# A two-layer transformer with cross-attention and a mixture of experts on one core: the plan of the side work rearranged

## The chip, the core and the metric

The kernel runs on one core of a Trainium2 chip. Such a core has five engines, each with a queue of its own that is worked off in order: TensorE (PE in the profile, its weight loads PEld), VectorE (DVE), ScalarE (ACT), GpSimd (POOL) and SyncE (SP), whose queue here issues DMAs. The metric is the device time of one execution in microseconds, the median of several runs; lower is better.

## The reference

64 sequences of 32 rows with 256 features (2048 rows in all), and a context of 257 rows for each sequence. Six steps, each added to `x` after a layer norm, cut to what matters:

```python
x = x + xattn0(norm(x), ctx)   # 16 heads of 16, rotary, window: first 32 context rows, causal
x = x + attn0(norm(x))         # 16 heads of 16, rotary, causal over the 32 rows
x = x + ffn0(norm(x))          # 256 -> 256, input rounded to fp8 with one scale a row
x = x + xattn1(norm(x), ctx)   # 16 heads, all 257 context rows, masked
x = x + attn1(norm(x))         # "mixer", below
x = x + moe(norm(x))           # 1 shared and 8 routed experts, 256 -> 512 -> 256, top 2

def mixer(x):
    gate = sigmoid(relu(x @ gate_w1 + b1) @ gate_w2 + b2)          # 64, then 32 features
    glob = gate * (x @ U_w) * cumsum(x @ V_w, axis=1)
    return conv3(x) + glob @ out_w + out_b

def moe(h):
    probs = softmax(h @ router_w + router_b)                       # 8 logits a row
    w = top-2 probs of a row, others 0
    return shared(h) + sum_e w[e] * expert_e(h)
```

## The kernel before

**Tiles.** The rows lie in SBUF as four groups `xs[g]` of four tiles of 128 rows (`NG = NT = 4`); a tile is four sequences. There are three stages: the two small attentions of layer 0 (to about 197 us), the big cross-attention of layer 1 (to about 688 us), and `mixture`, the experts with their routing.

**How order is made.** Inside the cross-attention and around it the engines' queues follow the order in which the Python code issues instructions, so the plan written out in the code is the plan that runs. The steps of side work (`linear`, `norm_steps`, `mixer`, `normed`) are generators: each `yield` ends a piece, and somebody calls `next` on them between the pieces of the main work. Work that is put off a little further goes to a list, `pending`, which `catch_up()` empties.

**The cross-attention's loop** (`cross_attention`, L1400 to L1459) runs over tiles `i` = 0 to 17 and pieces `b` = 0 to 3; the text calls one piece a tick, k = 4i + b. Three tiles are in flight: the keys of tile i+1, the scores of tile i, and values and context of tile i−1. A tick issues, in this order: four transposes `ps_t` and their copy `eT`; the weights' products put off from the tick before (POOL), `own_heads` and, at b = 1, `project` (`ps_p`); `catch_up()`; `run(k − 0.5)`; eight matmuls of values `ps_v`; four more `ps_t`; one piece of `side`; `run(k)`; `head_blocks` (`qb`, POOL) for a later tile and the keys `ps_k`; the scores `ps_s` in two halves, followed by four minima on the DVE (`e<-ps_s,mask`) and four exponentials on ACT; at b = 1 `last_keys` (`ps_le`, then `lv`); the context `ps_o`. A tick without side work lasts 5.67 us on PE.

**The side work of the loop** is `side_work(g + 1)`, begun at t = 0 of each group: the nine pieces of `linear` (norm, row maxima, scaling by the reciprocal, rounding to fp8 in two pairs with a helper tile `big`, sums `y`, `q`, transposes `ps_qT` in `by_feature`, matmuls `ps_ff` in `outputs`), the norm of the cross-attention, its transposes `psT`, and two matmuls of queries `ps_q`. `linear` of group 0 and the norm behind it are run by `first_sides()` between the last groups of layer 0 (L1481).

**The planned work.** `planned()` (L1032) puts the pieces of the mixers of finished groups and of the norms before the experts (`normed`: norm, store of `y` for the gathers, transposes `psT`, router matmuls `ps_r` of 8 columns, `lg`) at ticks. A mixer's pieces: statistics, two halves of the norm with `y` by ACT, transposes `psT`, the product `ps_huv` with the scan and product that make `hub` on the DVE, the gate `ps_g`, two `ps_d` with their convolution taps (`conv`), and two pairs of rows transposed back, `ps_x`, and added to `x`. A rank-one part of each norm, the reciprocal root, is a chain of twelve short instructions on POOL; the last ones use `eng = vector`, the DVE.

**PSUM.** All side tiles of the cross-attention (`ps_k`, `ps_v`, `ps_le`, `ps_p`, `psT`, `ps_qT`, `ps_ff`, `ps_q`, `ps_huv`, `ps_g`, `ps_d`, `ps_x`, `ps_r`) take turns in two banks through `shared_bank`: each waits for the reader of the tile before the last.

**The mixture** (L1526) issues the last mixer half (`mixer(3, range(2, 4), vector, False)`), the norms of group 3, the routing (`choose`) of the first 12 tiles and of the last 4, matmuls of the shared expert between them (`ps_sh`, `ps_so`), and then the 20 expert tiles. `last_pieces` holds what the plan leaves over: before, one norm, that of the first half of group 3.

Of the kernel before, what the change touches and what calls it, by code (L numbers as in the profile page):

```python
# [20 lines left out]
NG, NT = 4, 4  # L21
# [44 lines left out]
def perceiver_kernel(ctx: ExitStack, tc: tile.TileContext, a: dict, out: bass.AP):  # L66
# [619 lines left out]
    def catch_up():  # L686
        while pending:
            pending.pop(0)()

    def linear(g, by_act=False):  # L690

        x = xs[g]
        y = yield from norm_steps(g)

        for t in range(NT // 2):
            gpsimd.tensor_tensor(x[:, t], x[:, t], row(R_FF), ALU.add)
        yield
        am = small.tile([P, NT], F32, tag="am", name="am")
        vector.tensor_reduce(am, y, AX.X, ALU.max, apply_absolute_value=True)
        xsc = small.tile([P, NT], F32, tag="xsc", name="xsc")  # L700
        rsc = small.tile([P, NT], F32, tag="rsc", name="rsc")
        osc = small.tile([P, NT], F32, tag="osc", name="osc")

        def scales():
            vector.tensor_scalar(xsc, am, 1e-12, 1.0 / 448.0, ALU.max, ALU.mult)
            vector.reciprocal(rsc, xsc)
            vector.tensor_scalar(osc, xsc, vec[:, V_WS : V_WS + 1], None, ALU.mult)

        pending.append(scales)
        for t in range(NT // 2, NT):  # L710
            gpsimd.tensor_tensor(x[:, t], x[:, t], row(R_FF), ALU.add)
        yield

        def scaled(ts):
            for t in ts:
                if by_act:
                    scalar.activation(y[:, t], y[:, t], AF.Copy, scale=rsc[:, t : t + 1])
                else:
                    gpsimd.tensor_scalar(
                        y[:, t], y[:, t], rsc[:, t : t + 1], 1.0, ALU.mult, ALU.mult  # L720
                    )

        scaled(range(2 if by_act else NT))
        yield
        qs, qTs = [], []

        def rounded(pair):


            v = y[:, 2 * pair : 2 * pair + 2, :]  # L730
            big = sb.tile([P, 2, D], F32, tag="big", name="big")
            vector.tensor_scalar(
                big.bitcast(I32), v.bitcast(I32), 0x7F800000, None, ALU.bitwise_and
            )
            vector.tensor_scalar(big, big, 2.0**-6, 1.5 * 2.0**20, ALU.max, ALU.mult)
            q = sb.tile([P, 2, D], BF16, tag=f"fq{pair}", name="q")
            qs.append(q)

            def sums():
                vector.tensor_tensor(v, v, big, ALU.add)  # L740
                vector.tensor_tensor(q, v, big, ALU.subtract)

            pending.append(sums)

        def by_feature(pair):
            ps = shared_bank[0]([P, 2, 2 * P], "ps_qT", BF16)
            for c in range(2):
                for i in range(2):
                    turn(ps[:, c, i * P : (i + 1) * P], qs[pair][:, i, c * P : (c + 1) * P], ident_bf)
            qT = sb.tile([P, 2, 2 * P], BF16, tag=f"fqT{pair}", name="qT8")  # L750
            scalar.copy(qT, ps)
            qTs.append(qT)

        def outputs(pair):
            ps = shared_bank[0]([P, 2, D], "ps_ff")
            for i in range(2):
                proj(
                    ps[:, i, :],
                    lambda k: qTs[pair][:, k, i * P : (i + 1) * P],
                    lambda k: w8[:, k, :],  # L760
                )
            for i in range(2):
                t = 2 * pair + i
                x = xs[g][:, t, :]
                vector.scalar_tensor_tensor(
                    x, ps[:, i, :], osc[:, t : t + 1], x, ALU.mult, ALU.add
                )

        rounded(0)
        if by_act:  # L770
            scaled(range(2, NT))
        yield
        rounded(1)
        yield
        by_feature(0)
        yield
        by_feature(1)
        outputs(0)
        yield
        outputs(1)  # L780

# [11 lines left out]
    def mixer(g, ts, eng=None, by_act=True, early=False):  # L793
# [4 lines left out]
        steps = norm_steps(g, eng, True, ts, by_act, lent[:, 1] if early else None)  # L798
# [66 lines left out]
        for pair in range(n // 2):  # L865
            ps = shared_bank[0]([P, 2, D], "ps_x")
            for i in range(2):
                at = slice((2 * pair + i) * P, (2 * pair + i + 1) * P)
                for c in range(2):
                    turn(ps[:, i, c * P : (c + 1) * P], conv[c][:, at], ident)  # L870
            mine = x[:, t0 + 2 * pair : t0 + 2 * pair + 2, :]
            vector.tensor_tensor(mine, ps, mine, ALU.add)


    nt_all = NG * NT
# [145 lines left out]
    def fill_hidden(n):  # L1021

        for _ in range(n):
            shared_hidden(*next(hidden_units))
# [7 lines left out]
    def planned():  # L1032
        def at(piece, *turns):
            for k in turns:
                plan.setdefault(k, []).append(lambda: next(piece, None))

        plan[5] = [
            lambda: vector.tensor_scalar(
                half_b[64:96], vec[64:96, V_GB2 : V_GB2 + 1], 0.5, None, ALU.mult
            )  # L1040
        ]
        for g in range(2):
            k = 16 * g
            at(
                mixer(g, range(NT), early=True),
                *range(k + 24, k + 31), k + 33, k + 34, k + 36,
            )
        at(mixer(2, range(NT)), 53, 54, 55, 55, 56, 57, 58, 59, 60, 61)
        at(normed(0, range(NT)), 48, 51, 52, 54, 57, 58)
        at(normed(1, range(NT)), 56, 58, 59, 60, 62, 63)  # L1050
        at(mixer(3, range(2)), 60.5, 61, 62, 63, 64, 65, 66, 67)
        plan.setdefault(66, []).append(lambda: fill_hidden(1))
        at(normed(2, range(NT)), 62, 63, 64, 65, 66, 67)
        plan[65].append(lambda: fill_hidden(1))
        plan[66].append(lambda: fill_hidden(2))
        last_pieces.append(normed(3, range(2)))

    def run(k):
# [3 lines left out]
    last_pieces = []  # L1062


    def cross_attention(loaded):
# [28 lines left out]
        def key_tile(i):  # L1094
# [4 lines left out]

        own4 = fold[:, None, :].to_broadcast([P, 8, S])  # L1100
        of4 = sb.tile([P, 4, DH], F32, tag="of4", name="of4")
        vector.tensor_copy(
            of4, cst[:, C_B4 : C_B4 + 4][:, :, None].to_broadcast([P, 4, DH])
        )

# [3 lines left out]
        def last_rows(i, dst):  # L1109
            ps = pkv([P, 2, NB], "ps_l")  # L1110
            for c in range(2):
                proj(
                    ps[:, c, :],
                    lambda k: w[:, i, k, c * P : (c + 1) * P],
                    lambda k: lasts[:, k, :],
                )
            if i == 1:
                bias = vec[:, V_X1K : V_X1K + 2][:, :, None].to_broadcast([P, 2, NB])
                vector.tensor_tensor(dst, ps, bias, ALU.add)
            else:  # L1120
                vector.tensor_copy(dst, ps)

        def queries(yT, c, qT):
            ps = pkv([P, GT], "ps_q")
# [275 lines left out]
        for i in range(nt + 2):  # L1400
# [15 lines left out]
            qb_next = []  # L1416
            if i > nt:
                own_heads()
                next(last_pieces[0])
                project(done)  # L1420
            for b in range(4 if i <= nt else 0):
                if before is not None:
# [11 lines left out]
                if before is not None:  # L1434
                    v = values(before, b)
                    turned(before, b, 1, eT, i == nt - 1)
                    if b == 0:
                        spread(before)
                next(side, None)
                run(NT * i + b)  # L1440
                if after is not None:
                    if b == 0:
# [7 lines left out]
                    keys(after, b)  # L1450
                if now is not None:
                    weights = scores(now, b)
                if before is not None:
                    if b == 1:
                        last_keys(before)
                    own_heads = context(before, b, eT, v)
# [24 lines left out]
    def first_sides():  # L1481

        steps = linear(0, True)
        yield next(steps)
        yield
        yield next(steps)
        yield next(steps)
        yield next(steps)
        catch_up()
        yield next(steps)  # L1490
        yield
        yield next(steps)
        yield catch_up()
        yield next(steps)
        yield catch_up()
        yield next(steps)
        yield next(steps)
        finish(steps)
        yield
        steps = norm_steps(0, apart=True)  # L1500
        yield next(steps)
        yield next(steps)
        yield
        first_y.append(finish(steps))
        for t in range(NT):
            gpsimd.tensor_tensor(xs[0][:, t], xs[0][:, t], row(R_XO1), ALU.add)
# [19 lines left out]
    def mixture():  # L1526
# [25 lines left out]
        sync.dma_start(out=rc, in_=a["route"])  # L1552
        before_bf = sb.tile([P, 2, P], BF16, tag="fq0", name="before_bf")
        catch_up()
        first_norm = last_pieces[0]
        last_mixer = mixer(3, range(2, 4), vector, False)
        last_norm = normed(3, range(2, 4), vector, False)
        early, late = choose(0, nt - 4), choose(nt - 4, 4)
        warm = small.tile([P, 1], F32, tag="warm", name="warm")
        scalar.activation(warm, ident[:, 0:1], AF.Exp)  # L1560
        next(last_mixer)
        next(last_mixer)
        next(last_mixer)
        next(last_mixer)
        next(early)
        next(early)
# [550 lines left out]
```

## Time and profile before

| | us |
|---|---|
| median of 3 runs | 906.47 (905.58 to 909.12) |
| the profiled execution, its own time | 905.83 |
| its span | 904.1 |
| mean granted clock of PE | 0.99 |
| cross-attention's ticks without side work | 5.67 |
| idle time of PE in 197 to 251 | 6.8 of 54 |
| in 251 to 665 | 10.2 of 414 |
| in 665 to 747 | 12.1 of 82 |
| in 747 to 880 | 0.6 of 133 |

The times are those of the profiled execution; the span is what its records cover, and 1.73 us lie around it. A busy time in the profile counts overlapping instructions of one engine once. PE is the engine that is busy almost throughout, so its gaps, and what ends them, are what the order of the side work can change.

### The profile page before, as it was taken

Reading aid. Unit: us, or ns where it says so; the run is one execution under the profiler, and the core shown is the slowest. Engines: PE = TensorE matmul, PEld = TensorE weight load, DVE = VectorE, ACT = ScalarE, POOL = GpSimd, SP = SyncE. Lnnn points to the kernel's source line nnn. Section 1 sums busy time; section 2 is a strip of 40 time slices with the busy share of each in tenths; the row PEclk is TensorE's granted clock in tenths of the full one; section 3 lists DMA queues with packets and bytes.
Section 4 is the critical chain, followed back from the end, with each engine's and each line's share of the span. In section 5 each row is a group of like instructions: output and inputs, shape, how many; then the busy total and the mean of one; then the engine's idle time right before and its main releaser. Section 6 shows DMA issues by size and latency. Waiting matters only on the chain.

```text
span 904.1 us, 22827 instructions
## 1 busy us (share of the span) xinstructions
PE 849.3 (94%) x8699; PEld 582.2 (64%) x8699; DVE 579.9 (64%) x1706; ACT 438.6 (49%) x1133; POOL 507.4 (56%) x988
## 2 busy tenths in 40 slices
PE   5899999979899999999999999998997889999996
PEld 3466666655466666665666656665675548888886
DVE  6987777896777667775877757755754862111116
ACT  2566666664554555564455644664642232222224
POOL 3477777864775666584665744584740254555430
PEclk9999999999999999999999999999997999999999
DMA  7555433542111011110111101120010046777758
GB/s 238 145 137 138 99 90 104 136 135 89 54 55 39 17 53 55 53 55 12 42 54 54 54 4 51 54 72 1 26 36 1 24 156 202 236 236 233 215 187 284
DMA packets 66926, 88.77 MB, mean 98 GB/s; under 512 B 32480, under 2 KB 50688, under 8 KB 64768
## 3 DMA queue, kind: packets, MB, share of 16 engines
q1 hardware_dynamic: 63264, 77.73, 28.6%
q0 software_dynamic: 3456, 9.44, 3.1%
q8 instruction: 69, 1.13, 0.5%
q14 instruction: 41, 0.34, 0.1%
q10 hardware_dynamic: 96, 0.13, 0.1%
HBM read 65.78 MB, written 13.11 MB: 87 GB/s over the span
## 4 chain that ended last, share of the span: by engine, by line
PE 66%; DVE 17%; POOL 5%; ACT 5%; issue 3%; DMA 2%; SPq 0%; DVEq 0%; ACTq 0%; POOLq 0%
PE ps_v L119 11%; PE ps_o L119 11%; PE ps_k L119 9%; PE ps_h L119 7%; PE ps_t L122 6%; PE ps_qk L119 4%; PE ps_s L119 3%; PE ps_p L119 3%; PE ps_so L119 2%; ACT e L107 2%; PE ps_q L119 2%; POOL sq L107 1%; DVE y L107 1%; DVE x L107 1%; PE pair_bank L119 1%
## 5 line engine op out<-in xcount | busy, mean ns | idle before, releaser
L107 ACT ACTIVATE e<-e,xnm 128x257 f32<-128x257 f32 x256 | 127.2, 498 | 44.9 <-DVE xnm L107 44.3
L119 PE MATMUL ps_k<-ct,w_w_l1x 128*128 128x512 f32 x256 | 122.5, 601 | 3.0 <-DVE x L107 1.4
L107 POOL TENSOR_SCALAR e<-e,xsm 128x256 f32<-128x256 f32 x256 | 125.1, 508 | 0.0
L107 DVE CUSTOM_DVE_ANT_0 e<-ps_s,mask 128x257 f32<-128x257 f32 x256 | 93.7, 421 | 46.5 <-PE ps_s L119 45.7
L119 PE MATMUL ps_v<-w_w_l1x,ct 128*128 128x256 f32 x512 | 121.1, 379 | 0.0
L107 DVE COPY eT<-ps_t 128x512 f32<-128x512 f32 x124 | 85.2, 687 | 31.4 <-PE ps_t L122 31.3
L122 PE MATMUL ps_t<-cst,e 128*128 128x128 f32 x640 | 102.3, 282 | 2.2 <-DVE eT L107 1.9
L119 PEld LDWEIGHTS ps_v<-w_w_l1x,ct 128*128 128x128 f32 x512 | 93.5, 190 | 10.8 <-issue 0.2
L107 ACT ACTIVATE kT<-ps_k,vec 128x512 f32<-128x512 f32 x64 | 44.0, 688 | 105.5 <-PE ps_k L119 105.5
L107 POOL TENSOR_TENSOR x<-x,rows 128x256 f32<-128x256 f32 x96 | 70.0, 747 | 39.3 <-DVE y L107 27.7
L122 PEld LDWEIGHTS ps_t<-cst,e 128*128 128x128 f32 x640 | 71.8, 141 | 20.5 <-DVE eT L107 5.0
L107 ACT ACTIVATE hTr<-ps_h,w 128x256 f32<-128x256 f32 (+1 forms) x80 | 31.4, 449 | 104.7 <-issue 82.7
L107 DVE TENSOR_TENSOR og<-ps_o,b 128x512 f32<-128x512 f32 (+1 forms) x20 | 12.8, 638 | 105.6 <-PE ps_o L119 105.6
L119 PEld LDWEIGHTS ps_k<-ct,w_w_l1x 128*128 128x128 f32 x256 | 44.5, 190 | 44.7 <-issue 34.8
L1860 POOL DMA_INDIRECT r_rows<-og,lv x36 | 35.6, 989 | 59.1 <-DVE og L107 54.2
L107 ACT COPY v<-ps_v 128x512 f32<-128x512 f32 x80 | 46.4, 582 | 44.0 <-PE ps_v L119 43.6
L119 PE MATMUL ps_h<-ygT,w 128*128 128x256 f32 (+1 forms) x320 | 65.8, 359 | 0.1
L119 PE MATMUL ps_o<-w,hTr 128*128 128x256 f32 x288 | 65.3, 379 | 0.0
L107 POOL TENSOR_TENSOR last<-e,xsm 128x4 f32<-128x4 f32 x64 | 15.0, 234 | 81.1 <-DVE xsm L107 81.1
L119 PEld LDWEIGHTS ps_o<-w,hTr 128*128 128x128 f32 x288 | 54.4, 190 | 7.2
L119 PEld LDWEIGHTS ps_h<-ygT,w 128*128 128x128 f32 x320 | 54.9, 190 | 6.2 <-issue 0.3
L107 ACT ACTIVATE kb<-kT,cst 128x256 f32<-128x256 f32 x96 | 45.4, 512 | 25.2 <-POOL kT L107 23.6
(221 smaller groups left out, 1659.2 us busy)
## 6 DMA issues: line engine op xcount, KB each, us to landing
ct<-in_ctxT SPq DMA_DIRECT2D x16, 1024.0 KB, 5.5
w<-in_ew SPq DMA_DIRECT2D x20, 514.0 KB, 3.7
w<-in_ew SPq DMA_DIRECT2D x20, 512.0 KB, 3.6
far<-part SPq DMA_DIRECT2D x126, 64.0 KB, 2.3
v_rows<-v SPq DMA_DIRECT2D x16, 256.0 KB, 2.3
vb<-v_rows SPq DMA_DIRECT2D x64, 64.0 KB, 2.3
r<-r_rows SPq DMA_DIRECT2D x8, 512.0 KB, 8.4
b<-in_eb SPq DMA_DIRECT2D x20, 128.0 KB, 3.2
```

Of the source, the lines that this page charges most:

```text
L107: ins = getattr(self.engine, name)(*args, **kw)
L119: return kept(nc.tensor.matmul(ps, **args))
L122: return kept(nc.tensor.transpose(ps, src, eye))
L1860: wrote = nc.gpsimd.indirect_dma_start(out=r_rows, out_offset=bass.IndirectOffsetOnAxis(ap=write_i[:, at : at + 1], axis=0), in_=o[:, i, : ...
```

## The change

All parts of it reorder work or give it to another engine; no matmul is added or removed.

- `linear`: `outputs(0)` comes ahead of `by_feature(1)`. `first_sides` calls the pieces of it in other turns (`catch_up()` later), and two copies in `cross_attention` (`of4` and the last values `vl`) go from VectorE to ScalarE.
- In the loop's first tile (i = 0) the side piece comes behind `scores`, where it came before `run` and the keys.
- `mixer`: a `yield` stands between the two pairs of rows, so the second pair's `ps_x` is one piece of its own, and the plan has a turn more for it. In the plan of groups 0 and 1 the turn k+29 is left out, and the hub's piece goes to k+30, the gate's to k+31.
- Mixer 2 begins at 52.5 (with two pieces at 54), norm 0's transposes go to 55 and its router to 57, norm 1's pieces to 54, 55, 57, 58 and 59, and norm 2's to 62 to 65.
- Norm 1's last piece (router) and norm 2's last two (transposes, router) are left to `mixture`, which calls them between the pieces of `last_mixer`.

The diff, cut to its core:

```diff
@@ linear
+        outputs(0)
         by_feature(1)
-        outputs(0)
         yield
         outputs(1)
@@ mixer
             vector.tensor_tensor(mine, ps, mine, ALU.add)
+            if pair == 0:
+                yield
@@ planned
                 mixer(g, range(NT), early=True),
-                *range(k + 24, k + 31), k + 33, k + 34, k + 36,
-            )
-        at(mixer(2, range(NT)), 53, 54, 55, 55, 56, 57, 58, 59, 60, 61)
-        at(normed(0, range(NT)), 48, 51, 52, 54, 57, 58)
-        at(normed(1, range(NT)), 56, 58, 59, 60, 62, 63)
+                *range(k + 24, k + 29), k + 30, k + 31, k + 33, k + 34, k + 36, k + 37,
+            )
+        norms = [normed(g, range(NT)) for g in range(3)]
+        at(mixer(2, range(NT)), 52.5, 53, 54, 54, 55, 56, 57, 58, 59, 60, 61)
+        at(norms[0], 48, 51, 52, 54, 55, 57)
+        at(norms[1], 54, 55, 57, 58, 59)
         at(mixer(3, range(2)), 60.5, 61, 62, 63, 64, 65, 66, 67)
         plan.setdefault(66, []).append(lambda: fill_hidden(1))
-        at(normed(2, range(NT)), 62, 63, 64, 65, 66, 67)
+        at(norms[2], 62, 63, 64, 65)
...
+        last_pieces.extend(norms[1:])
         last_pieces.append(normed(3, range(2)))
@@ cross_attention
-        vector.tensor_copy(
+        scalar.copy(
             of4, cst[:, C_B4 : C_B4 + 4][:, :, None].to_broadcast([P, 4, DH])
         )
...
-                vector.tensor_copy(dst, ps)
+                scalar.copy(dst, ps)
...
-                next(last_pieces[0])
+                next(last_pieces[2])
...
-                next(side, None)
+                if i > 0:
+                    next(side, None)
                 run(NT * i + b)
...
                     weights = scores(now, b)
+                if i == 0:
+                    next(side)
@@ first_sides
         yield catch_up()
-        yield next(steps)
-        yield catch_up()
+        yield
         yield next(steps)
         yield next(steps)
+        catch_up()
+        yield next(steps)
+        yield
         finish(steps)
-        yield
         steps = norm_steps(0, apart=True)
@@ mixture
-        first_norm = last_pieces[0]
+        norm_1, norm_2, first_norm = last_pieces
...
         next(last_mixer)
+        next(norm_2)
         next(last_mixer)
+        next(norm_1, None)
         next(last_mixer)
+        next(norm_2, None)
         next(last_mixer)
```

## The prediction, made before the changed kernel was run

> **What bounds the kernel.** I read the page first, then busy time by stage, then what the matmul engine (PE) waits for, then the timeline around each edit. From the page:
>
> ```profile
> span 904.1 us, 22827 instructions
> PE 849.3 (94%) x8699; PEld 582.2 (64%) x8699; DVE 579.9 (64%) x1706; ACT 438.6 (49%) x1133; POOL 507.4 (56%) x988
> PE 66%; DVE 17%; POOL 5%; ACT 5%; issue 3%; DMA 2%; SPq 0%; DVEq 0%; ACTq 0%; POOLq 0%
> ```
>
> PE is busy for 849.3 of 904.1 us, so at most 55 us can be had by reordering. The table by stretch (length, then each engine's busy time, then granted clock) says where:
>
> ```profile
> 197.00:251.00 54.00, 47.23 (x542) 26.97 (x541) 38.55 (x121) 28.48 (x78) 30.50 (x71) 1.00 0.28 91
> 251.00:665.00 414.00, 403.77 (x4388) 259.93 (x4386) 292.01 (x982) 225.78 (x645) 256.82 (x614) 1.00 0.13 41
> 665.00:747.00 82.00, 69.91 (x395) 44.45 (x393) 51.85 (x162) 24.92 (x39) 23.76 (x41) 0.92 0.19 61
> 747.00:880.00 133.00, 132.36 (x676) 116.87 (x675) 23.50 (x40) 31.38 (x80) 63.94 (x66) 1.00 0.71 221
> ```
>
> The change touches the first three: 6.8, 10.2 and 12.1 us of idle PE. After 747 PE is full and nothing is edited. PE's waits (line, releaser: sum, times, longest):
>
> ```profile
> PE psT L122 <- DVE y L107: 7.1, 4, 4.3
> PE ps_c L122 <- DVE o L107: 3.1, 3, 1.4
> PE psT L122 <- DVE hub L107: 2.6, 1, 2.6
> PE ps_k L119 <- DVE x L107: 1.4, 2, 1.0
> PE ps_le L119 <- DVE hub L107: 1.4, 2, 0.7
> ```
>
> Four of the change's targets are here: `hub`, `x` (pair of rows), `o` (first group), and the 4.3 us before the last mixer's transposes.
>
> **The change, part by part.** PE issues the same matmuls before and after; only their order and waits differ, so each part is a difference of waits (+ is slower). A PE gap costs about 0.17 us more than its idle time in lost overlap of the neighbours.
>
> *First group, layer 0's end (n=7).* Two copies (`of` 0.61, `vl` 0.28) leave the DVE for ACT, and the roundings move back a turn, so that DVE's `o` comes earlier: gaps of 1.39 (at 198.63) and 1.17 (at 203.19) shrink by about 1.4 together. But the second `ps_qT` now waits for the rounding's `q` in the same turn, about 204.6, and the keys start at 205.05 instead of 205.44: 0.4 is left of the 1.4. In the next turn the second `ps_ff`'s two scalings (0.88) stand on the DVE queue, until about 212.85, ahead of the BN statistics that began at 210.95. POOL's chain (12 steps, 213.32 to 216.62) and `y` (217.32) follow them: `psT` ends 1.3 later. I take +1.3, that is with the 0.4 already lost behind this wait; bounds +0.3 and +1.5.
>
> *Tile 0, side pieces behind the minima.* The four minima of a piece no longer stand behind `linear`'s DVE work: the gaps of 1.76 (231.55) and 0.48 (235.87) go down by 0.6 in all. In return the norm's statistics come behind the minima, POOL's chain begins near 233.6 instead of 230.2, and POOL is full from 237.5 to 256.5. The second `qb` ends near 248.4 instead of 247.6, and the second half of the scores at k=4, which waits for it already (0.26), waits 0.8 longer. The minima win nothing that outlasts it: +0.8, bounds +0.3 and +1.3.
>
> *`outputs(0)` ahead of `by_feature(1)`, k=8, 24, 40.* Two banks take turns. The timeline of PE, ACT and DVE at k=8:
>
> ```profile
> 270.12 0.39 PE L122 MATMUL ps_qT<-ident_bf,q 128*128 128x128 bf16 x4
> 270.54 0.58 ACT L107 COPY qT<-ps_qT 128x512 bf16<-128x512 bf16 x1
> 270.57 0.60 PE L119 MATMUL ps_ff<-w,qT 128*128 128x256 bf16 x4
> 271.18 1.98 PE L119 MATMUL ps_k<-ct,w_w_l1x 128*128 128x512 f32 x4
> 271.21 0.88 DVE L107 SCALAR_TENSOR_TENSOR x<-ps_ff,osc,x 128x256 f32<-128x256 f32 x2 [0.19 <-PE ps_ff L119]
> ```
>
> Before, `ps_k` takes `ps_qT`'s bank, free at 271.12 by ACT. After, it takes `ps_ff`'s, whose readers are the two scalings: the DVE's `eT` copy ends at 271.02, they end at 271.9, and the keys start 0.77 later. Three groups: +2.3, bounds +1.0 (if the half tick after regains the rest) and +2.6.
>
> *Hub one tick later (k=30, 46 instead of 29, 45).* The hub's DVE scan no longer stands before `lv` and the minima of its old tick; 0.68 and 0.68 before `ps_le` go, about 0.1 each comes back beside them. −1.2, bounds −1.5 and −0.6.
>
> *Pair of rows in two turns.* Before, the second pair's four transposes need the first pair's reader and then `ps_k` needs both additions: 1.00 at 462.86. Split over k=36 and 37, each tick has one addition to hide behind `ps_t`: −0.75. (The twin at k=52, 0.44 at 576.03, is counted below.) Bounds −1.2 and 0.
>
> *k=52 to 62.* Mixer 2's piece starts half a tick earlier, norm 0's transposes go to k=55, norm 1's pieces one to three ticks earlier. Before, at k=57, the four transposes of norm 0 are caught by the mixer's scan and hub product:
>
> ```profile
> 611.81 1.40 DVE L107 TENSOR_TENSOR_SCAN sums<-cst,ps_huv 32x128 f32<-32x128 f32 x4 [1.74 <-ACT hub L107]
> 613.24 0.69 DVE L107 SCALAR_TENSOR_TENSOR hub<-sums,ps_huv 32x512 f32<-32x512 f32 x1
> 614.07 0.63 PE L122 MATMUL psT<-cst,y 128*128 128x128 f32 x4 [2.58 <-DVE hub L107]
> ```
>
> That is 2.58 + 0.17; with 0.50 at k=56 (0.16 and 0.34) and 0.4 of the pair, 3.7 go, and about 1 us of smaller ones (0.66 at 650.76, 0.32 at 654.04). Against it: six activations of `y` at k=54 (0.51 each) push ACT's copies of four `psT` at k=55, about 1.5; `psT` at k=59 waits for a conv step, 0.6. Tick by tick the eleven sum to 77.0 us against 79.5: −2.5. No row shows that crowding, so the bounds are wide, −3.7 and −1.0.
>
> *Two norms in the mixture.* Norm 1's router (1.85 at 654.54), norm 2's `psT` (0.96) and router (1.88) move behind k=67, where the DVE's chain for the last mixer (statistics, three Newton steps of three instructions of 0.16, `y`) leaves PE idle:
>
> ```profile
> 688.07 1.10 PE L119 MATMUL ps_p<-w_w_l1x,own 128*128 128x256 f32 x4 [0.95 <-DVE own L107]
> 693.48 1.13 PE L122 MATMUL psT<-cst,y 128*128 128x128 f32 x4 [4.31 <-DVE y L107]
> 695.29 2.07 PE L119 MATMUL ps_huv<-yT,narrow 128*128 128x256 f32 x4 [0.67 <-ACT yT L107]
> ```
>
> 4.7 us of PE work fit into 4.31 + 0.95 of idle time; −4.4. The DVE takes two `lg` additions (0.19 each) into its chain, inside the rounding; the cover of it all is that gap, and without it the part is worth 0. The stores of norm 0's and 1's `y` on SP's queue and POOL's four additions to `x` (2.79 together at 594.50) move with the pieces; nobody reads the stores before the mixture's gathers (`ps_yg` waits 1.0 for one, after the routing), so I take 0. Bounds −4.7 and −1.5.
>
> *The granted clock.* It was half in 656.56 to 659.97, just after the sixteen narrow router matmuls at 654.54; PE work of that stretch cost about 1.35 more (the `ps_s` 1.16 against 0.69, `ps_o` 1.08 against 0.65, `ps_t` 1.06 against 0.66). With that router gone I count −0.9, two thirds of it; bounds −1.35 and 0. The row: PE was busy 3.09 of the 3.41 us before the drop, with 1.85 of router matmuls of 8 columns. The Trainium skill, "TensorE: Matmul & The Clock Gate", What's actually happening, has half clock after an idle window of about 3.4 us; by that alone this busy window should have kept full clock, and the drop would have to be explained by the narrow matmuls counting little. The trace's window length, 3.41, agrees.
>
> Sum: 1.3 + 0.8 + 2.3 − 1.2 − 0.75 − 2.5 − 4.4 − 0.9 = −5.35. The profiled execution took 905.83 us (span 904.1 and 1.73 around it), which gives 900.5. The median of the runs, 906.47, is 0.64 above it; against that the forecast is 906.47 − 5.35 = **901.1**, given as 901.0.
>
> **Rivals.**
>
> *A: the gains are eaten.* The three plain losses (+4.4) are read from single queues and hardly fail; the gains of −2.5 and −4.4 rest on crowded ticks that no row shows. With both at their poor bounds (−1.0, −1.5) the sum is 4.4 − 1.2 − 0.75 − 1.0 − 1.5 − 0 = −0.05: 906.4. For it: DVE is at 52 of 82 busy in 665 to 747 and in order. Against: in the 4.3 us only the DVE works (POOL has 21.6 us of idle time before 693.41, ACT 8.6 before 694.65).
>
> *B: half clock through the mixture (the other side).* The clock was half at 690.69 to 700.93 and 714.58 to 718.00, and back between. After the change 32 router matmuls of 8 columns and eight transposes stand where PE idled. It decides if these hold the clock at half as the idle time did, and longer: the window 653.15 to 656.56 shows that narrow matmuls can. From about three half windows more on, 700.93 to 714.58, with 10.68 us of PE work, runs at half too. Eight `ps_so` at half (697.15) took the 3.62 that sixteen took at full clock (707.46), so its 5.5 us of `ps_so` cost 5.5 more, `ps_d`, `ps_x`, `psT` and `ps_r` some 1.5, and the −0.9 isn't won: 901.0 + 7.9 = 908.9. Against: the `ps_so` at 697.15 did bring full clock at 700.93. The Trainium skill, same page, Part 4: PE-mode transpose, says that transposes don't count as busy as other matmuls do; by it, filling a gap with transposes doesn't save the clock. The trace can't separate it here: `psT` and routers come mixed.
>
> *C: the change doesn't reach its gap.* PE takes the refill, but the last mixer's `y` (DVE, 692.92) now stands behind the two `lg` additions, which wait for PE's routers and ACT's `yT`. If these end more than 2 us after the old `y`, only about 2.4 of the 4.4 is won and the clock's 0.9 is lost with it: 903.9.
>
> **Chances.** Forecast as summed (899 to 902.5) 0.50; C 0.17; A 0.17; B 0.09; better than summed (bounds on the good side, −9, 897.5) 0.07. What a measurement can tell from no change is about 0.5%, 4.5 us: faster is below 901.9, slower above 911.0. Faster: most of the forecast's case (0.40), the better case (0.07), and a little of C (0.06): 0.53. Slower needs B with some of A's poor bounds (0.06), or a crowding past them (0.02): 0.08. The rest, 0.39, is the same. The range leaves out the best tail and part of B: 897.0 to 907.5.
>
> **What would show it.** PE gaps at k=29, 36, 45 and 57 gone; a new wait `ps_k` on DVE `x` three times near 0.8; the first `psT` of layer 1 later by about 1.3 relative to its keys; ticks 52 to 62 shorter by 2.5; the gap before the last mixer's `psT` under 1 us, and that stage (665 to 747) no longer by itself than before, though 4.7 us of work has entered it. The forecast is wrong if k=55 grows by over 3 us, if the new gap at `ps_k` is not there, or if 665 to 747 keeps a granted clock under 0.92 with the last mixer's `psT` still waiting over 2 us for `y`.

## The result, and the profile after

| | us | ratio to the kernel before (95%) | mean granted clock, median of the runs |
|---|---|---|---|
| before, 22 runs | 908.01 | | 0.984 to 0.986 in the four groups of 9 to 17 runs beside the experiments |
| after, 22 runs | 904.66 | 0.9966 (0.9954 to 0.9979) | 0.984 |
| after, profiled execution | 904.31, span 902.5 | | 0.981 |

The change wins 0.34%, 3.1 us (1.9 to 4.2), where 5.35 us had been forecast: faster, but by less than the 0.5% that the forecast had called likelier. From the page of the changed kernel:

```profile
span 902.5 us, 22832 instructions
PE 856.0 (95%) x8699; PEld 586.3 (65%) x8699; DVE 579.8 (64%) x1704; ACT 439.6 (49%) x1135; POOL 505.5 (56%) x988
PE 71%; DVE 13%; ACT 5%; POOL 5%; issue 3%; DMA 2%; SPq 1%; DVEq 0%; ACTq 0%; POOLq 0%
```

PE issues the same 8699 matmuls, yet is busy 6.7 us longer (849.3 before): the same work ran slower, at a mean granted clock of 0.981 against 0.990. The profiled execution of before had a better clock than most of its runs, whose medians lie at 0.984 to 0.986, so not every stretch of half clock that only the new profile has belongs to the change. The table by stretch shows where the clock fell (the column after the five engines):

```profile
197.00:251.00 54.00, 47.20 (x491) 26.10 (x493) 37.14 (x112) 25.98 (x69) 24.76 (x58) 0.95 0.28 91
251.00:665.00 414.00, 405.02 (x4432) 260.95 (x4433) 295.84 (x991) 228.74 (x654) 259.38 (x623) 1.00 0.13 41
665.00:747.00 82.00, 74.33 (x414) 48.19 (x413) 52.42 (x164) 25.12 (x39) 26.26 (x45) 0.92 0.19 62
```

At the end of layer 0 the clock fell from 1.00 to 0.95; after 665 it is 0.92 as before, over fewer gaps. In the first 35 us, which the change does not touch, it is 0.90 here and was 1.00 before. PE's waits in the changed kernel:

```profile
PE psT L122 <- DVE y L107: 3.2, 5, 1.2
PE ps_k L119 <- DVE x L107: 2.7, 3, 0.9
PE ps_qT L122 <- DVE q L107: 2.0, 1, 2.0
PE ps_o L119 <- DVE own L107: 1.6, 1, 1.6
PE ps_c L122 <- DVE o L107: 0.7, 2, 0.5
```

The 4.3 us of `psT` are gone, and so are `hub` at 2.6 and 1.4; three waits of `ps_k` near 0.9 and one of `ps_qT` are new. PE's timeline at the two places that decide most, the end of layer 0 and the mixture:

```profile
205.46 0.40 PE L122 MATMUL ps_qT<-ident_bf,q 128*128 128x128 bf16 x4 [2.01 <-DVE q L107]
205.69 3.58 PE L119 MATMUL ps_k<-ct,w_w_l1x 128*128 128x512 f32 x4
...
685.13 1.10 PE L119 MATMUL ps_p<-w_w_l1x,own 128*128 128x256 f32 x4 [0.95 <-DVE own L107]
686.07 1.34 PE L122 MATMUL psT<-cst,y 128*128 128x128 f32 x8
687.35 4.12 PE L119 MATMUL ps_r<-narrow,yT 128*128 128x8 f32 x32
691.32 1.09 PE L122 MATMUL psT<-cst,y 128*128 128x128 f32 x4
```

The four matmuls of `ps_k` behind the 2.01 us wait took 3.58 us, where 1.88 is usual: the clock was half from 205.84 to 209.25. In each profile the stretches of half clock begin on a grid of steps of 3.41 us, and last one, two or three of them; such a step is called a window below. In the mixture the three moved pieces fill the gap, and the last mixer's `psT` follows without a wait.

A tick's start is that of its first `ps_t`. Against the profile of before, the changed kernel's profile is late (+) or early (−) by: +3.45 at k=4, +6.18 at k=9, +6.06 at k=33, +4.84 at k=48, +2.87 at k=63, −1.0 at `ps_rank` in the mixture, −1.6 at the end. From k=9 on it gains much as forecast; the start loses more.

### The profile page after: what moved, and what is told of

Same layout as the page of the kernel before. It is cut to its first block, busy times and chain, and to the rows that moved or that the text cites. A ratio compares the mean times of both kernels' runs of the same rounds, so it can differ in the third digit from the quotient of the medians.

```text
span 902.5 us, 22832 instructions
## 1 busy us (share of the span) xinstructions
PE 856.0 (95%) x8699; PEld 586.3 (65%) x8699; DVE 579.8 (64%) x1704; ACT 439.6 (49%) x1135; POOL 505.5 (56%) x988
## 3 DMA queue, kind: packets, MB, share of 16 engines
q8 instruction: 69, 1.13, 0.6%
## 4 chain that ended last, share of the span: by engine, by line
PE 71%; DVE 13%; ACT 5%; POOL 5%; issue 3%; DMA 2%; SPq 1%; DVEq 0%; ACTq 0%; POOLq 0%
PE ps_o L119 11%; PE ps_v L119 11%; PE ps_k L119 10%; PE ps_h L119 7%; PE ps_t L122 6%; PE ps_qk L119 5%; PE ps_p L119 4%; PE ps_s L119 3%; ACT e L107 2%; PE ps_so L119 2%; PE ps_sh L119 2%; PE ps_q L119 2%; POOL sq L107 1%; PE pair_bank L119 1%; DVE x L107 1%
## 5 line engine op out<-in xcount | busy, mean ns | idle before, releaser
L119 PE MATMUL ps_k<-ct,w_w_l1x 128*128 128x512 f32 x256 | 126.1, 616 | 3.9 <-DVE x L107 2.7
```

Of the source, the lines that this page charges most:

```text
L119: return kept(nc.tensor.matmul(ps, **args))
```

## Experiments

All are timed against the kernel before on the same chip.

| run | what it is | us | ratio (95%) |
|---|---|---|---|
| undo_first | after, first-group part undone | 898.71 | 0.9918 (0.9900 to 0.9936) |
| undo_tile0 | after, tile 0's side pieces undone | 904.48 | 0.9975 (0.9966 to 0.9985) |
| undo_order | after, order in `linear` undone, groups 1 to 3 | 901.93 | 0.9942 (0.9924 to 0.9960) |
| undo_three | all three undone | 896.43 | 0.9882 (0.9867 to 0.9898) |
| undo_two | undone but for tile 0's pieces | 900.34 | 0.9904 (0.9879 to 0.9930) |
| mixture_only | before, two norms in the mixture | 902.80 | 0.9942 (0.9921 to 0.9964) |
| first_filler | after, PE's wait filled | 902.09 | 0.9936 (0.9912 to 0.9960) |
| wide_router | undo_three, router 72 columns | 892.32 | 0.9831 (0.9811 to 0.9850) |
| before_wide | before, router 72 columns | 905.17 | 0.9971 (0.9954 to 0.9988) |
| after_wide | after, router 72 columns | 897.59 | 0.9891 (0.9862 to 0.9919) |
| wide_tile0 | wide_router, tile 0's pieces behind the minima | 893.60 | 0.9846 (0.9818 to 0.9873) |
| wide_copies | wide_router, two copies on ScalarE | 892.85 | 0.9833 (0.9809 to 0.9857) |
| wide_first | wide_tile0 with the first-group part | 896.67 | 0.9890 (0.9871 to 0.9909) |
| wide_filler | wide_first, PE's wait filled | 894.81 | 0.9868 (0.9847 to 0.9889) |
| wide_ff_early | wide_first, second `ps_ff` a slot earlier | 897.30 | 0.9882 (0.9863 to 0.9901) |
| wide_turns | wide_first, copies back on VectorE | 896.99 | 0.9879 (0.9860 to 0.9898) |

### The three losing parts, undone one by one

undo_first takes back the hunk of `first_sides`, the two `scalar.copy`, and for group 0 (where `by_act` is true) the order in `linear`:

```diff
-        outputs(0)
+        if not by_act:
+            outputs(0)
         by_feature(1)
+        if not (not by_act):
+            outputs(0)
```

> The changed kernel with its first-group part undone (turns of first_sides, order of linear's last pieces for group 0, the two copies back on VectorE). Theory 'order': in the changed kernel the transposes of the norm end 4.1 us later than before at the end of layer 0, in every execution: 2 us of waiting on ps_qT for q gathers PE's idle time in one place, the clock drops for 3.4 us behind it, and the norm's chain starts later. Undone, 904.66 - 4.1 = 900.6, ratio to the kernel before 0.992. Rival 'chance': the two half-clock windows at 195.6 and 205.8 belong to the one profiled execution; the part costs the forecast's 1.3, so 903.4, ratio 0.995. Neither expects it to be slower than the changed kernel.

It came out as "order" said: 0.9918 where 0.992 was named, so the part costs 0.0048, 4.35 us (2.4 to 6.4 by the two intervals), and not 1.3. The median granted clock of its runs is 0.990, that of the changed kernel 0.984. In its profile the norm's last `psT` ends 29.2 us after the first `ps_l`, to 0.03 as in before; in the changed kernel 33.3.

> The changed kernel with by_feature(1) ahead of outputs(0) again for groups 1 to 3 (ticks 8, 24, 40). Theory 'order': the three new waits of ps_k for the scalings (0.89 each in the changed kernel's trace, 0.67 net a tick) go: 904.66 - 2.0 = 902.7, ratio 0.9944. Rival: something behind takes up part of it (the half tick's minima or eT), 903.7, ratio 0.9955.

`if by_act: outputs(0)` ahead of `by_feature(1)`, and otherwise behind it. 0.9942 against 0.9966: 2.2 us, and each of the ticks 8, 24 and 40 is 6.84 again instead of 7.51. The wait is the one that was named. The interval would hold the rival's 0.9955 too; the three ticks, 2.0 us together with nothing given back behind them, speak against it:

```profile
276.08 0.38 PE L122 MATMUL ps_qT<-ident_bf,q 128*128 128x128 bf16 x4
276.44 0.86 DVE L107 SCALAR_TENSOR_TENSOR x<-ps_ff,osc,x 128x256 f32<-128x256 f32 x2
277.36 1.98 PE L119 MATMUL ps_k<-ct,w_w_l1x 128*128 128x512 f32 x4 [0.89 <-DVE x L107]
```

This is k=8 of the changed kernel: `ps_k` starts when the two scalings have ended, not with ACT's copy (276.51 to 277.09).

> The changed kernel with only the side pieces of tile 0 back ahead of the keys. Theory 'order': from the end of layer 0 to k=8 the changed kernel loses 1.4 (ps_t waits 1.04 for xsm at k=4 and 0.89 for eT at k=7, ps_s 0.75 for qb, against 0.7 won at the minima); undone, 904.66 - 1.4 = 903.3, ratio 0.995. Rival: it was right as it stands once the norm is late, since the minima no longer wait behind side work; undone 904.7 or up to 0.7 more, ratio 0.9966 to 0.9975.

`next(side, None)` stands ahead of `run` for every tile again. By time this is 0.0009 slower than the changed kernel, within the intervals, while its profile is 2.0 ahead at k=8. But that lead is there before tile 0 begins: the norm's `psT` ends 31.31 after `ps_l` instead of 33.32, since here the wait for `q`, again 2.01, is followed by no half clock (`ps_k` takes 1.94). From the end of that `psT` to the values of k=9 the two differ by only 0.2 (57.5 and 57.7), with a half-clock window at 234.4 to 237.8 that the other has not. So this run does not decide what tile 0's edit costs.

> All three undone; what is left of the change are the ticks 29 to 67 and the two norms in the mixture. Theory 'order': the three add up, 4.1 + 1.4 + 2.0 = 7.5, so 897.2, ratio 0.988. Rival 'chance': 1.3 + 0.8 + 2.0 = 4.1, so 900.5, ratio 0.992. By the changed kernel's trace the remaining parts win 1.5 + 1.6 + 2.0 + 4.9 = 10, some of it given back to a second half-clock window near 711.

Together 0.9882, as "order" said: the rest of the change is worth 10.7 us.

> The changed kernel with the first-group part and the order of linear's last pieces undone, tile 0's side pieces still behind the minima. By the ticks of undo_first (k=8 at +1.32 over before) and undo_three (+0.90), tile 0's edit costs 0.4 to 1.4 net, so this is that much slower than undo_three: 897 to 898, ratio 0.989 to 0.990. Rival, from undo_tile0's time (0.9975, no gain where 1.4 was expected): the edit wins 0.8, so 895.7, ratio 0.9873.

0.9904 is a little above the 0.989 to 0.990 that was expected, with an interval that holds it but not the rival's 0.9873. Against undo_three the difference, 0.0022, is still within the intervals. wide_tile0 asked again where the clock disturbs less:

> wide_router (0.9831) with tile 0's side pieces behind the minima. By the ticks (k=4 to k=8) of the profiles the edit wins 0.6 at the minima and loses 1.2, 0.1 and 0.75 at k=4, 6 and 7: 1.4 to 1.5 slower, ratio 0.9847. Rival, from undo_tile0's time: 0.8 faster, 0.9822.

0.9846, and 893.6 us against 892.3: 1.3 us slower, as the ticks say. From the end of the norm's `psT` to the values of k=9 it is 55.5 us without the edit (before, undo_three, wide_router, wide_copies) and 57.0 with it (wide_tile0, wide_first, wide_filler). The intervals alone would not show it; the ticks do, seven times alike (and 57.1 to 57.3 in undo_two and wide_ff_early, which have the edit too).

### The gain in the mixture, alone

In before, `normed(1)` is planned at 56, 58, 59, 60, 62 and `normed(2)` at 62 to 65; the rest is called in `mixture`, as in the change.

> The kernel before with only norm 1's router, and norm 2's transposes and router, moved into the mixture. Theory: the three pieces' 4.7 us of PE work fit into the last mixer's gap, and 5.8 are won up to ps_p, 0.8 given back at the last mixer's psT, 1 to 1.7 at the half-clock windows behind the narrow router matmuls: -3.5 to -4.5, ratio 0.995 to 0.996. Rival A of the prediction (the refill fails): -1.5, ratio 0.998.

0.9942, 5.3 us (3.3 to 7.2): a little better than expected. That it is the forecast's 4.4 + 0.9 to the tenth is luck, but both causes are seen: in its profile the refilled gap is gone, and so is the window at 656, while the two windows of the mixture (688.0 to 694.9, 708.5 to 715.3) last 13.65 us together, as before.

### What makes the clock drop

first_filler adds, for group 0 and ahead of the second `ps_qT`:

```diff
+            if by_act and pair == 1:
+                for _ in range(28):
+                    turn(ps[:, 0, 0:P], ident_bf, ident_bf)
```

> The changed kernel with 28 extra bf16 transposes of the identity on PE, into the same PSUM tile ahead of the second ps_qT of group 0, inside the 2.0 us that ps_qT waits for q (their results are overwritten; nothing else is changed). Theory 'order': about 2 of the 4.1 us that the first group's part costs come from the half clock behind this wait (ps_k at 205.69 took 3.58 for 1.88, its followers late by as much). If transposes keep the clock up, ps_k takes 1.9 again and the kernel gains 1.7 to 2: 902.8, ratio 0.9945, and the mean clock rises by about 0.002. Rival, the Trainium skill's statement ('TensorE: Matmul & The Clock Gate', Part 4: PE-mode transpose) that transposes do not count as busy: no window goes, the time stays at 904.7, ratio 0.9966. Second rival, that the drop comes from this part of the kernel being late for other reasons: the same as no change.

PE's timeline of this kernel:

```profile
204.68 1.73 PE L122 MATMUL ps_qT<-ident_bf 128*128 128x128 bf16 x28
206.86 0.40 PE L122 MATMUL ps_qT<-ident_bf,q 128*128 128x128 bf16 x4 [0.45 <-DVE q L107]
207.09 1.94 PE L119 MATMUL ps_k<-ct,w_w_l1x 128*128 128x512 f32 x4
```

`q` comes no earlier, but `ps_k` takes 1.94 instead of 3.58. Of the seven profiles with this part and no filler, six have a half-clock window that begins between 204.4 and 205.8; the two with filler have none, and of the nine without the part one has (wide_copies). The seventh, undo_tile0, has the same wait, but the border of two windows at 203.69 falls into it, so that less of the idle time lies in one window. The windows in question, in after, undo_tile0 and first_filler (after the length, PE's busy time):

```profile
202.43:205.84 3.41, 1.26 (x11) 0.95 (x12) 3.34 (x8) 1.42 (x4) 2.00 (x3) 1.00 0.92 332
203.69:207.10 3.41, 1.77 (x8) 0.86 (x8) 2.33 (x4) 0.62 (x2) 2.69 (x3) 1.00 0.80 279
203.70:207.11 3.41, 2.74 (x40) 2.47 (x39) 3.34 (x7) 1.56 (x4) 1.86 (x3) 1.00 1.06 344
```

In the two with filler the whole wait lies in one window, as in the six but wide_ff_early, so the border isn't what saved them. In the six, PE was busy 0.87 to 1.46 us of the window before the half one; in before, 2.10. That is no rule for every place: in before, a window with 1.52 busy (612.18 to 615.59) was followed by full clock. By time first_filler is 0.9936 against 0.9966, 2.7 us, with intervals that barely overlap; wide_filler has 2.0, with intervals that do, and 2.96 busy in its window. So transposes seem to have kept the clock up here, by two profiles out of two and by times that lean the same way. The Trainium skill ("TensorE: Matmul & The Clock Gate", Part 4: PE-mode transpose) says that they don't count as busy in the same way and that full clock doesn't engage for them; these two runs disagree, and the measurement decides.

> undo_three with the router's matmuls 72 columns wide instead of 8 (the 64 columns of U and V beside the router's are multiplied as well and left unread). Theory 'narrow': the half-clock windows in 615 to 717 follow the runs of router matmuls because these hardly occupy PE; 72 columns take the same time a matmul (bound by the weight load, 0.116 each) and keep the clock up: one to three windows of 3.4 us go, each worth 0.7 to 1.7: 893 to 895, ratio 0.985 to 0.987. Rival 'idle': the windows follow PE's gaps (0.95 at ps_p, 0.67 at ps_huv and ps_r), nothing changes, 0.9882. Second rival: the wider matmuls take longer (32 x 0.05 = 1.6 more) and win nothing: 0.990.

```diff
-        ps = shared_bank[0]([P, n, NE], "ps_r")
+        ps = shared_bank[0]([P, n, 64 + NE], "ps_r")
...
-                lambda k: narrow[:, k, N_RW : N_RW + NE],
+                lambda k: narrow[:, k, N_RW - 64 : N_RW + NE],
...
-            ps,
+            ps[:, :, 64:],
```

This gave the fastest kernel of the study, 892.32 us, 0.5% below undo_three and 1.7% below before. The mean clock of its runs is 0.997 in the median, and this is its timeline in the mixture:

```profile
677.93 3.79 PE L119 MATMUL ps_r<-narrow,yT 128*128 128x72 f32 x32
681.56 0.60 PE L122 MATMUL psT<-cst,y 128*128 128x128 f32 x4
682.84 1.13 PE L119 MATMUL ps_huv<-yT,narrow 128*128 128x256 f32 x4 [0.68 <-ACT yT L107]
683.81 1.89 PE L119 MATMUL ps_so<-w_shared,hT 128*128 128x256 f32 x8
```

Nine times as many columns cost nothing (sixteen took 2.00 in before_wide, 1.95 before), while `psT` takes 0.60 for 1.09, `ps_huv` 1.13 for 2.07 and `ps_so` 1.89 for 3.08 in the changed kernel. The gaps around them, 0.95 and 0.68, are the same as ever, so the rival "idle" falls for this kernel.

> The changed kernel with the router's matmuls 72 columns wide. Theory 'narrow': what wide_router won over undo_three (0.9882 to 0.9831) is won here too, 0.005: ratio 0.9915; the windows at 619, 690 to 697 and 711 to 718 go, those at 195.6 and 205.8 stay, mean clock 0.990. If the gain depended on the other undone parts, 0.994 or more.

0.9891: 6.8 us less than the changed kernel, more than the 4.6 expected, which the intervals (4.0 to 9.6) hold too. Its profile also lacks the window at 195.6, far from any router.

> The kernel before with the router's matmuls 72 columns wide, as in wide_router. Theory 'narrow': the windows behind routers (656.6 and 714.6 in the profile of before, and the length of the one from 690.7) go, the one behind the idle 4.3 us stays for one window: 3 to 5 us won, ratio 0.9945 to 0.9965, mean clock 0.988 to 0.992. Rival: in the kernel before the windows come from PE's idle time in the mixture, as the 4.31 us gap stands there: 0 to 1.5 won, ratio 0.998 to 1.

0.9971, 2.6 us: less than expected. The window from 692.9 to 699.7 stays in its profile, two windows long, behind the 4.31 us gap that is idle there (PE is busy for 0.00 us from 689.5 to 692.9). The two causes are thus both real, idle time and narrow matmuls; which of them holds a window depends on the kernel.

### What the first group's part is made of

> wide_tile0 (0.9846) with the first-group part of the change in place (turns, order for group 0, copies). If the part costs 4.35 whatever the clock does elsewhere: 897.8, ratio 0.9894. If 2.1, as after_wide suggests: 0.987.

0.9890: the higher figure, 0.0044 above wide_tile0, 4.0 us (0.7 to 7 by the two intervals). Against this base:

> wide_first with 28 extra transposes of the identity inside the wait of ps_qT for q. Theory: the half window behind that wait (204.5 or 205.8 in three profiles) goes, ps_k takes 1.9 instead of 3.4 to 3.6: 1.5 to 1.7 less than wide_first. Rival: the window is lost only now and then, by its phase: 0 to 0.7 less.

2.0 less (0.9868), as expected, if with overlapping intervals. In its profile the norm's `psT` ends 31.3 after `ps_l`, against 32.2 in wide_first and 29.2 without the part, and this with a half window at 195.4 that wide_first had not, and that makes the keys start 0.7 later.

> wide_first with the second ps_ff of group 0 right behind the second ps_qT, one slot earlier, so that its two scalings stand ahead of the next turn's softmax on VectorE and the norm's statistics follow the turn's x at once. Theory 'chain': psT's wait for y (1.05 + 0.28 + 0.34) shrinks by 1.3 to 1.6; PE then waits for qT's copy (0.6 to 0.7) before ps_ff, in the place where it is not covered: net 0.6 to 1.2 less than wide_first. Rival: the added wait makes the window behind it idle and nothing is won.

`finish(steps)` stands ahead of the empty `yield`. The rival holds: `psT`'s waits for `y` shrink from 1.06, 0.28 and 0.34 to 0.13 and 0.34, `ps_ff` waits 0.68 for `qT` instead, two half-clock windows follow (204.4 to 211.2), and `psT` ends 32.2 after `ps_l` as before the edit. 0.9882 is no difference that the intervals show.

> wide_first with the two copies back on VectorE: of (0.61) stands ahead of y and q again. Theory 'race': q then starts after GpSimd's second qT, GpSimd is not held up (1.3 instead of 1.73), PE's gap at pair_bank is 1.27 instead of 1.70 and its window keeps full clock more often, but o is 0.6 later in the next turn: 0.2 to 1 less than wide_first. Rival: VectorE is what bounds this stretch, and the copies' 0.9 on it come through: 0.5 to 0.9 more.

0.9879, not told apart from 0.9890. PE's gap at `pair_bank` is 1.40 instead of 1.70. Whether the copies cost anything by themselves was asked too:

> wide_router (0.9831) with nothing but the two copies of the first-group part on ScalarE. Theory 'lock': without the of copy (0.61) ahead of it VectorE's q starts before GpSimd's second qT instead of behind it (193.18 against 193.26 in the changed kernel; 193.59 against 193.30 before), so GpSimd is the one that waits (1.73 against 1.31 to 1.38) and PE's gap at pair_bank grows from 1.27 to 1.69; where that leaves its window idle, the clock is half for 3.4 us at 195.6. Cost 0.4 to 1.5: ratio 0.9835 to 0.985. Rival: the copies only free VectorE, which is busy here: o is earlier by 0.6 to 0.9, twice, and 0.5 to 1 is won, ratio 0.982.

No cost shows: 0.9833 against 0.9831, but the intervals hold the 0.4 to 1.5 us of the theory. In the profile a half window at 205.4 follows PE's gaps, and the norm's `psT` ends 30.5 after `ps_l`, 1.3 later than in wide_router. The race that was suspected is there, and is decided by 0.02 to 0.3 us. In the changed kernel VectorE is first and GpSimd is held up; in before it was the other way:

```profile
193.18 0.69 DVE L107 TENSOR_TENSOR q<-y,big 128x512 bf16<-128x512 f32 x1
193.26 1.73 POOL L107 TENSOR_TENSOR qT<-near,far 128x512 f32<-128x512 f32 x1 [0.67 <-DMA far<-part]
```

```profile
193.59 1.64 DVE L107 TENSOR_TENSOR q<-y,big 128x512 bf16<-128x512 f32 x1
193.30 1.38 POOL L107 TENSOR_TENSOR qT<-near,far 128x512 f32<-128x512 f32 x1 [0.59 <-DMA far<-part]
```

In wide_copies GpSimd began 0.02 us ahead (194.13 against 194.15), `q` took 1.79, and PE waited 1.13, so there the copies alone didn't make VectorE the first. The Trainium skill ("SBUF — State Buffer", Who interferes with whom) has one port pair shared by the two engines, and issue order deciding who blocks; these rows agree.

## Why the prediction was wrong, and where it was right

| step | forecast | measured | by |
|---|---|---|---|
| first group | +1.3 | +4.0 to +4.35, each give or take 2 to 3 | undo_first, wide_first |
| tile 0 | +0.8 | +1.3 to +1.5 | wide_tile0, ticks |
| order in `linear` | +2.3 | +2.0 to +2.2 | undo_order, ticks |
| hub | −1.2 | −1.5 | ticks 29 to 31, 45 to 47 |
| pair of rows | −0.75 | −1.1 | ticks 36, 37 |
| k=52 to 62 | −2.5 | −2.0; −3.3 to −3.6 where no half window falls there | ticks |
| mixture and clock | −4.4 − 0.9 | −5.3 | mixture_only |

With 4.35, 1.4, 2.1, −1.5, −1.1, −2.0 and −5.3 the sum is −2.0; measured are −3.1 (−1.9 to −4.2).

**The step that failed is the first group's +1.3: it counted waits alone and put the clock there at nothing.** The waits were read rightly, and their size too. wide_first is the profile of this part without a half window ahead of the wait. In it the keys (`ps_k`) start 13.80 us after `ps_l` instead of 14.50, so they do come earlier; from the `pair_bank` behind them to the norm's statistics it is 6.06 instead of 3.69, for the second `ps_ff` and its scalings now stand in between; 0.30 of slack behind the statistics goes, and from keys to `pair_bank`, where the clock holds, 0.06 is lost (1.87 for 1.81). That is −0.70 + 2.37 − 0.30 + 0.06 = +1.43.

The rest is half clock. The gathered idle time, 2.01 us in one place where it had been 1.39, 1.17 and 0.71, made its window idle enough for the clock to drop: from the keys to `pair_bank` it is then 3.5 us (after, undo_order, wide_first), and 1.87 where it did not drop (undo_tile0, first_filler, wide_filler), 1.6 more. And six of the nine profiles with the part (one of the nine without) have a window that begins between 194.9 and 196.9; in after, undo_order, undo_tile0 and the two with filler the keys start 0.7 to 1.06 later than in wide_first. With both windows the changed kernel's `psT` is 4.14 late, with one wide_first's is 3.03. The forecast had looked for the clock only at 656 and in the mixture.

**Smaller.** Tile 0 lost more than its bound of +1.3: 1.2 at k=4 and 0.75 at k=7, where `ps_t` waits 1.04 for `xsm` and 0.89 for `eT`, neither of them in the list of waits that the step had named; the one that it had, `ps_s` for `qb`, grew from 0.26 to 0.75. The crowding at k=55 was overrated: that tick grew by 2.7, but 2.0 of it is the moved `psT` and only 0.3 is waiting. Against that a router moved to k=57 cost 1.6 in the profiled execution, as the next `ps_k` took 3.44 at half clock.

**Right.** The three `ps_k` waits, the end of the gaps at k=29, 36, 45 and 57, and the refill of the last mixer's gap came as worked out. Rival C did not happen. Nor did rival A's: the gains were not eaten, a loss was sized too small. Rival B is right in its cause, wrong in its place: narrow router matmuls do hold the clock down, for 690.5 to 697.4 and 711.0 to 717.8, but between them it was full, and the 13.65 us at half are as many as before had there; after_wide puts the price of narrow routers over the whole changed kernel at 6.8 us (4.0 to 9.6). The −9 of the better case is not the sum of the good bounds, which is −10.85; nothing hangs on it.

**Open.** Why a given execution has a window at 195 or at 222 and another has none isn't settled, nor what in the first group's part brings on the one at 195 (PE's gap at `pair_bank`, 1.70 for 1.27, is the nearest candidate); the windows lie 3.41 us apart and start anywhere against the kernel. What tile 0's edit does to the changed kernel itself rests on the ticks; the time of undo_tile0 shows no gain.

## What to carry to other kernels

Where a moved step gathers PE's idle time into one place, price the clock behind it as well as the wait: here 2 us of waiting cost 1.6 us more. And ask whether the base's profile had a usual clock: this one had 0.990, the median of its runs 0.984 to 0.986. When steps are moved on an in-order queue, follow each later chain from the instruction that starts it, and add the delays along it; done so, the waits came out at +1.43 where +1.3 was forecast. Where narrow matmuls follow each other no faster than wider ones would (here one in 0.11 us with 8 columns and with 72), widen them with columns that lie beside them.

## What the runs showed of the hardware

Sixteen fp32 matmuls 128x128 by 8 columns and the same by 72 took 1.95 and 2.00 us, but behind two of the three places with narrow ones in undo_three the granted clock was half for 6.8 us (682.2 to 689.0, 702.6 to 709.5), behind the wide ones of wide_router nowhere: mean clock of the profiles 0.997 against 0.987, 892.32 us against 896.43. In the two profiles where bf16 transposes filled 1.7 us of a 2.0 us wait, the clock behind it stayed full; in six of seven without them it did not.
